# Graph transformer on one core: when output rows are written, and where q and the attention weights stand in PSUM

## The chip, the cores and the metric

The kernel runs on one core of a Trainium2 chip as one program. The metric is the device time of one execution in microseconds (us). Three timed runs of the kernel before gave 2392.58, 2392.24 and 2391.94 us; their median, 2392.24 us, is the time that the change is measured against. The execution that the profiler recorded is a separate one and took longer (below).

## The reference

There are 3327 nodes with 256 features, and an adjacency matrix of 3327 x 3327 with about 16 neighbours in a row. Layer 0 is a single-head graph attention over this matrix. Layers 1 to 3 are transformer layers whose attention is masked by the same matrix (8 heads of 32, feed-forward width 1024):

```python
def layer(x, adj, w_qkv, w_proj, b_proj, w1, b1, w2, b2, g1, be1, g2, be2):
    q, k, v = split(layer_norm(x, g1, be1) @ w_qkv)          # 3 x (n, heads, 32)
    scores = einsum('nhd,mhd->hnm', q, k) * SCALE
    attn = softmax(where(adj != 0, scores, -inf), axis=-1)
    x = x + einsum('hnm,mhd->nhd', attn, v).reshape(n, 256) @ w_proj + b_proj
    return x + gelu(layer_norm(x, g2, be2) @ w1 + b1) @ w2 + b2
```

The output is x after layer 3, in the order of the input's rows.

## The kernel before, in words

Layer 0 reads the whole adjacency matrix, and in passing makes for each node a list of its neighbours. Nodes are then sorted by their number of neighbours and cut into 26 blocks of 128 rows, so that a block needs only as many neighbour places (`CAPS`, 9 to 34) as its fullest row. Everything after that works on the sorted blocks; `perm` holds each row's original number.

Layers 1 to 3 each run over the blocks in the order 24, 23, ..., 0, 25 (`ORDER`). A block's neighbour places are cut into groups of up to four (`cuts`), and one group is one turn: 118 turns in a layer. Five engines share a turn:

- GpSimd (POOL) gathers. `gather` (L759) sends one indirect DMA for each neighbour place: 128 rows of keys and values (2 KB each) from `kv` in HBM to one of 12 slots in SBUF; 430 gathers in a layer. A loop in `layer` (L878) sends them up to four groups ahead of the group in hand, while slots are free.
- VectorE (DVE) multiplies the keys by q (L778), sums over each head (L779), takes the maximum and subtracts it (L785 to L788, in `exps`), and later multiplies the values by the weights (L811).
- ScalarE (ACT) takes the exponent (L789), copies the block's q into PSUM (L757, `place_q`), moves the summed values out (L820) and does the activations of the feed-forward part (L693).
- TensorE (PE) sums the weighted values of a block by transposing them into one PSUM accumulation (L814), and does all projections: `w_proj` (L665), `w1` (L689), `w2` (L702), and q, k, v of the next layer (L183, L188).
- SyncE (SP) loads q (L753, `load_q`) and stores k, v and q for the next layer (L728, L729).

The attention of a block overlaps that of the next one: while block k's scores are made, block k-1 has its softmax shares (`shares`, L791) and its values (`values`, L804). When a chunk of two blocks has its values, a generator `tail` (L652) is put on the list `tails`; each call of `turn` (L827) lets every tail that is due go one step on: projection, addition to x (L668), layer norm, whose power -0.5 is done by POOL (L137), feed-forward, addition to x (L708), and then q, k, v of the next layer.

The order of all this is written out by hand: under `manual_schedule`, each engine's instructions stand in the order in which the Python code issues them, and each engine takes its own queue in order. An instruction that waits therefore holds up all that stands behind it on its engine.

Two places matter here.

First, PSUM for q. The pool `ps_q` has two buffers of one PSUM bank each, and the blocks take turns in them. A block's q is copied into columns 0 to 255 (L757), all its keys are multiplied by it, and then `shares` writes the weights over q in the same columns (L798, L799), where `values` reads them. The buffer is free for block k+2 when block k has all its values. `place_q` of block k+1 is therefore issued when block k-1 has its last values, behind that block's L820, in the last turn but one of block k (L895, L896):

```python
                            if before.vdone == len(before.cuts) and k + 1 < NB:
                                att[k + 1].place_q()
```

Second, the output. In layer 3 a tail ends with the rows of its chunk, two turns after the addition L708 (L710): POOL writes one block after the other with an indirect DMA into `out`, 128 rows of 1 KB, by the row numbers in `perm` (L713). All 26 writes name the whole tensor `out`, so each waits until the one before it has landed. These writes stand in POOL's queue between the gathers: 22 of the 26 ahead of layer 3's last gather, always two in succession.

After layer 3 a few instructions work out a flag (L936) for whether the neighbour lists were large enough; a general path, not run here, would otherwise recompute everything.

Of the kernel before, what the change touches and what calls it, by code (L numbers as in the profile page):

```python
# [8 lines left out]
FP = mybir.dt.float32  # L9
# [6 lines left out]
PSUM = bass.MemoryType.PSUM  # L16
# [37 lines left out]
AHEAD = 3  # L54
NODES = 4
EARLY = 3
FH = FF // P // 2


# [5 lines left out]
def kernel(ctx: ExitStack, tc: tile.TileContext, ins, out: bass.AP):  # L65
# [563 lines left out]
    with ExitStack() as st:  # L629
# [3 lines left out]
        slots = st.enter_context(tc.tile_pool(name="slots", bufs=SLOTS))  # L633
        ps_g = st.enter_context(tc.tile_pool(name="ps2_g", bufs=4, space=PSUM))
        ps_o = st.enter_context(tc.tile_pool(name="ps2_o", bufs=2, space=PSUM))
        ps_q = st.enter_context(tc.tile_pool(name="ps2_q", bufs=2, space=PSUM))

        def gen(name):
            return ps_g.tile([P, 512], FP, tag="g", name=name)

        x_sb = keep.tile([P, NB, D], FP, name="x_sb")
        def node_x(b):
            nc.scalar.copy(x_sb[:, b, :], nodes_[b][:, :D])

# [7 lines left out]
        def tail(L, w, wqn, blocks, oT):  # L652


            n = len(blocks)
            b0 = blocks[0]
            tag = f"{L}_{b0}"
            xi = x_sb[:, b0:b0 + n, :]
            views = [x_sb[:, b, :] for b in blocks]
            pp = gen(f"pp_{tag}").rearrange("p (b d) -> p b d", d=D)  # L660
            nc.tensor.matmul(pp[:, :n, :], ones3,
                             bsum[:, 2 * L - 2, None, :].to_broadcast([3, n, D]), start=True, stop=False)
            for j in range(n):
                for c in range(2):
                    nc.tensor.matmul(pp[:, j, :], oT[:, c, j * P:(j + 1) * P], w["w_proj"][:, c, :],  # L665
                                     start=False, stop=(c == 1 and j == n - 1))
            yield 1
            nc.vector.tensor_add(xi, xi, pp[:, :n, :])  # L668
            mv, rs = variances(views, f"f{tag}")
            yield 2  # L670
            powers(rs, n)
            yield AHEAD - 1
            xns = normed(work, views, mv, rs, f"f{tag}")
            yield 1
            fT = work.tile([P, 2, 2 * P], FP, tag="fT", name=f"fT_{tag}")
            turned(gen, fT, xns, *gains(L, 1), f"f{tag}")
            yield 1
            pd = None
            while hidden:
                yield 1  # L680
            hidden.append(tag)
            for h in range(2):
                gT = work.tile([P, FH, 2 * P], FP, tag="gT", name=f"gT_{tag}_{h}")
                for f0 in range(0, FH, 2):
                    pu = gen(f"pu_{tag}_{h}_{f0}").rearrange("p (a r) -> p a r", a=2)
                    for a in range(2):
                        f = h * FH + f0 + a
                        for c in range(2):
                            nc.tensor.matmul(pu[:, a, :n * P], w["w1"][:, c, f * P:(f + 1) * P],  # L689
                                             fT[:, c, :n * P], start=(c == 0), stop=(c == 1))  # L690
                    for a in range(2):
                        f = h * FH + f0 + a
                        nc.scalar.activation(gT[:, f0 + a, :n * P], pu[:, a, :n * P], AF.Gelu_apprx_tanh,  # L693
                                             bias=pv[:, L - 1, 8 + f:9 + f])
                yield 1
                if h == 0:
                    pd = gen(f"pd_{tag}").rearrange("p (b d) -> p b d", d=D)
                    nc.tensor.matmul(pd[:, :n, :], ones3,
                                     bsum[:, 2 * L - 1, None, :].to_broadcast([3, n, D]), start=True, stop=False)
                for j in range(n):  # L700
                    for f in range(FH):
                        nc.tensor.matmul(pd[:, j, :], gT[:, f, j * P:(j + 1) * P], w["w2"][:, h * FH + f, :],  # L702
                                         start=False, stop=(h == 1 and f == FH - 1 and j == n - 1))
                if h == 0:
                    yield 1
            hidden.remove(tag)
            yield 1
            nc.vector.tensor_add(xi, xi, pd[:, :n, :])  # L708
            if L == LAYERS[-1]:
                yield 2  # L710
                for b in blocks:
                    r = ROWS[b]
                    nc.gpsimd.indirect_dma_start(  # L713
                        out=out, out_offset=bass.IndirectOffsetOnAxis(ap=perm[:r, b:b + 1], axis=0),
                        in_=x_sb[:r, b, :], in_offset=None)
                return
            mv, rs = variances(views, f"h{tag}")
            yield 2
            powers(rs, n)
            yield AHEAD - 1  # L720
            xns = normed(work, views, mv, rs, f"h{tag}")
            yield 1
            hT = work.tile([P, 2, 2 * P], FP, tag="fT", name=f"hT_{tag}")
            turned(gen, hT, xns, *gains(L + 1, 0), f"h{tag}")
            yield 1
            for j, b in enumerate(blocks):
                kv, q = qkv_rows(work, gen, wqn, hT[:, :, j * P:(j + 1) * P], L + 1, f"{L + 1}_{b}")
                nc.sync.dma_start(kv_dr[L + 1][b * P:(b + 1) * P, :], kv)  # L728
                nc.sync.dma_start(q_dr[L + 1][:, b, :], q)  # L729
                if j < n - 1:  # L730
                    yield 1
# [7 lines left out]
        class Attend:  # L739


            def __init__(self, L, b):
                self.L, self.b, self.tag, self.S = L, b, f"{L}_{b}", CAPS[b]
                self.cuts = cuts(b)
                self.tiles = []
                self.vdone = 0

            def load_q(self):
                if self.L == LAYERS[0]:
# [3 lines left out]
                    nc.sync.dma_start(self.q, q_dr[self.L][:, self.b, :])  # L753

            def place_q(self):
                self.qp = ps_q.tile([P, 512], FP, tag="qp", name=f"qp_{self.tag}")
                nc.scalar.copy(self.qp[:, :D], self.q)  # L757

            def gather(self, g):  # L759
                a, z = self.cuts[g]  # L760
# [8 lines left out]
            def scores(self, g):  # L769
                a, z = self.cuts[g]  # L770
                n = z - a
                if g == 0:
                    self.sc = work.tile([P, LW, HEADS], FP, tag="sc", name=f"sc_{self.tag}")
                if self.L == LAYERS[0]:

                    nc.scalar.copy(idx[:, self.b, a:z], self.tiles[g][:, :n, 2 * D])
                kq = self.tiles[g][:, :n, :D]
                nc.vector.tensor_mul(kq, kq, self.qp[:, None, :D].to_broadcast([P, n, D]))  # L778
                nc.vector.tensor_reduce(self.sc[:, a:z, :],  # L779
                                        kq.rearrange("p s (h d) -> p s h d", h=HEADS), AX.X, ALU.add)  # L780

# [9 lines left out]
            def shares(self):  # L791
                S = self.S
                scs = self.sc[:, :S, :]
                sm = work.tile([P, HEADS], FP, tag="sm", name=f"sm_{self.tag}")
                nc.vector.tensor_reduce(sm, scs.rearrange("p s h -> p h s"), AX.X, ALU.add)
                nc.vector.reciprocal(sm, sm)

                self.pw = self.qp[:, :LW * HEADS].rearrange("p (s h) -> p s h", h=HEADS)  # L798
                nc.vector.tensor_mul(self.pw[:, :S, :], scs, sm[:, None, :].to_broadcast([P, S, HEADS]))  # L799
                self.po = ps_o.tile([P, 2, P], FP, tag="po", name=f"po_{self.tag}")  # L800
                nc.tensor.matmul(self.po.rearrange("p c r -> p (c r)"), zeros_bf[:, :P], zeros_bf,
                                 start=True, stop=False)
# [20 lines left out]
        place = {b: (m, j) for m, blocks in enumerate(CHUNKS) for j, b in enumerate(blocks)}  # L823
        tails = []
        hidden = []

        def turn():  # L827

# [7 lines left out]
        def layer(L):  # L836
# [14 lines left out]
            att[0].load_q()  # L851
            att[0].place_q()
            att[1].load_q()
            before = None

            def part(a):
# [10 lines left out]
            for k, a in enumerate(att):  # L867
# [3 lines left out]
                for g in range(n):  # L871
# [10 lines left out]
                    a.scores(g)  # L882
                    if g == n - 1:
                        a.exps()
                    turn()
                    if k == NB - 1:
                        turn()
                    if before is not None:
                        if g == 0:
                            before.shares()  # L890
                        goal = max(g + 1, -(-len(before.cuts) * (g + 1) // max(n - 1, 1)))
                        while before.vdone < min(goal, len(before.cuts)):
                            part(before)
                            held -= 1
                            if before.vdone == len(before.cuts) and k + 1 < NB:  # L895
                                att[k + 1].place_q()  # L896
                    elif g == n - 1:
                        att[1].place_q()
                    now += 1
                before = a  # L900
            before.shares()
            while before.vdone < len(before.cuts):
                part(before)
                turn()
            while tails:
                turn()

        with tc.manual_schedule():
            for L in LAYERS:
# [191 lines left out]
```

## Time and profile before

| | |
|---|---|
| timed runs, median (lowest to highest) | 2392.24 us (2391.94 to 2392.58) |
| the profiled execution, its own time | 2871.28 us |
| its span, first to last instruction | 2869.2 us |
| mean granted TensorE clock in it | 0.753 |
| layer 0 and lists, to the first gather of layer 1 | 411 us |
| gathers of layer 1, first to last | 411 to 1186 us |
| gathers of layer 2 | 1262 to 1988 us |
| gathers of layer 3 | 2067 to 2803 us |
| the end, after the last gather | 67 us |

The profiled execution is 479 us longer than the median of the timed ones. Its durations are read as durations of single instructions; its waits belong to it alone, and how far the timed runs have them too has to be argued.

How to read the lines that follow: a row of the costliest groups gives the source line, the engine, the operation, out<-in, the count, then busy us and mean ns of one, then the idle time of the engine just before these instructions and who ended it. A row of waits gives the engine and line that waited, what released it, the sum in us, how many times, and the longest. A row of a stretch gives its limits, its length, and the busy time of each engine with its number of instructions. A row of the timeline gives start, length, engine, line, operation, and in brackets the idle time before it and who ended it. "issue" means that nothing in the profile explains the idle time; "remote" is a releaser that the trace does not hold.

### The profile page before, as it was taken

The page shows a single profiled execution, that of the slowest core. Times are in us where ns is not written, and L with a number is a line of the kernel's source. Part 1 is how long each engine was busy: PE and PEld are TensorE (multiplying, and loading weights), DVE is VectorE, ACT ScalarE, POOL GpSimd, SP SyncE. Part 2 cuts the span into 40 slices and gives each one's busy share as a digit, 9 for nine tenths or more (in the row PEclk, how much of TensorE's full clock was granted, in tenths as well). Part 3 has the DMA queues.
Part 4 walks back from the last instruction along what each step waited for, and adds up shares of the span by engine and source line. Part 5 has one row for each costly group of instructions (what it writes and reads, how often), then busy time and mean ns, then how long its engine had stood idle before and what let it go on. Part 6 is the DMA issues. An engine that isn't in the chain of part 4 may idle for free.

```text
span 2869.2 us, 26077 instructions
## 1 busy us (share of the span) xinstructions
PE 1716.9 (60%) x8346; PEld 1327.7 (46%) x8346; DVE 1756.5 (61%) x3214; ACT 776.2 (27%) x1564; POOL 1430.0 (50%) x1614
## 2 busy tenths in 40 slices
PE   7677622455666666752576676666725555566556
PEld 6555411444454444642454555554514444444445
DVE  5777735665667776725565755767246467555664
ACT  4777510123322222220232222122302222111112
POOL 0232345554456665336555556664165555665561
PEclk9889855677877667885687777777957777676768
DMA  5667155555456665345545556565255555555451
GB/s 211 218 179 223 59 137 165 151 172 148 129 156 187 178 183 169 109 154 170 148 146 158 174 162 191 169 182 151 99 175 161 155 152 155 168 172 152 145 170 30
DMA packets 165082, 453.04 MB, mean 158 GB/s; under 512 B 37711, under 2 KB 64985, under 8 KB 161609
## 3 DMA queue, kind: packets, MB, share of 16 engines
q0 software_dynamic: 107104, 350.26, 41.8%
q1 hardware_dynamic: 56652, 98.53, 10.9%
q10 hardware_dynamic: 1180, 2.49, 0.3%
q8 instruction: 69, 1.13, 0.2%
q14 instruction: 77, 0.63, 0.1%
HBM read 410.86 MB, written 40.29 MB: 157 GB/s over the span
## 4 chain that ended last, share of the span: by engine, by line
PE 32%; another core or an unknown queue 18%; DVE 17%; issue 15%; ACT 6%; POOL 6%; DMA 5%; DVEq 0%; ACTq 0%; SPq 0%; POOLq 0%
PE pd L702 8%; PE pu L689 7%; PE po L814 5%; PE pk L183 4%; DVE sl L778 4%; DVE sl L811 4%; POOL sl L764 3%; PE pp L665 3%; DVE sc L779 2%; DMA kv<-kvr 2%; DMA sl<-kv,idx 2%; PE pq L188 2%; ACT gT L693 1%; ACT L693 1%
## 5 line engine op out<-in xcount | busy, mean ns | idle before, releaser
L764 POOL DMA_INDIRECT sl<-kv,idx x1290 | 1229.0, 953 | 544.0 <-issue 355.4
L814 PE MATMUL po<-ident,sl 128*128 128x128 f32 x2580 | 471.7, 346 | 568.1 <-DVE sl L811 302.4
L778 DVE TENSOR_TENSOR sl<-sl,qp 128x1024 f32<-128x1024 f32 (+1 forms) x354 | 396.3, 1119 | 568.4 <-ACT qp L757 484.3
L814 PEld LDWEIGHTS po<-ident,sl 128*128 128x128 f32 x2580 | 395.6, 180 | 634.2 <-DVE sl L811 360.3
L702 PE MATMUL pd<-w,gT 128*128 128x256 f32 x1248 | 336.1, 427 | 165.4 <-ACT gT L693 112.6
L779 DVE TENSOR_REDUCE sc<-sl 128x32 f32<-128x1024 f32 (+1 forms) x354 | 398.2, 1125 | 29.5 <-remote 10.5
L689 PE MATMUL pu<-fT,w 128*128 128x256 f32 (+1 forms) x1344 | 328.6, 402 | 127.9 <-issue 66.4
L811 DVE TENSOR_TENSOR sl<-sl,qp 128x1024 f32<-128x1024 f32 (+1 forms) x354 | 388.9, 1119 | 8.1 <-DVE qp L799 3.5
L702 PEld LDWEIGHTS pd<-w,gT 128*128 128x128 f32 x1248 | 261.2, 215 | 228.0 <-ACT gT L693 127.1
L689 PEld LDWEIGHTS pu<-fT,w 128*128 128x128 f32 x1344 | 266.0, 213 | 176.2 <-issue 72.3
L693 ACT ACTIVATE gT<-pu,pv 128x256 f32<-128x256 f32 (+1 forms) x336 | 133.1, 456 | 374.5 <-remote 175.3
L137 POOL TENSOR_TENSOR rsig_f<-rsig_f,mhalf 128x2 f32<-128x2 f32 (+1 forms) x42 | 29.1, 693 | 339.6 <-DVE rsig_f L133 337.6
L820 ACT COPY oT<-po 128x256 f32<-128x256 f32 x78 | 29.1, 373 | 617.3 <-remote 228.6
L183 PE MATMUL pk<-wq,hT 128*128 128x512 f32 x312 | 169.6, 670 | 19.8 <-ACT hT L165 18.6
L708 DVE TENSOR_TENSOR x_sb<-x_sb,pd 128x512 f32<-128x512 f32 (+1 forms) x42 | 27.2, 648 | 207.2 <-PE pd L702 144.9
L608 DVE MAX8 cand<-abf 128x8 f32<-128x256 bf16 x338 | 118.2, 411 | 1.3 <-DMA node<-cand 1.1
L665 PE MATMUL pp<-w_proj,oT 128*128 128x256 f32 x312 | 94.1, 452 | 35.6 <-ACT oT L820 26.3
L165 ACT ACTIVATE fT<-pn_f,pv 128x256 f32<-128x256 f32 (+1 forms) x84 | 41.6, 545 | 249.2 <-remote 155.1
L693 ACT ACT_TABLE_LOAD x48 | 61.6, 1283 | 151.9 <-remote 88.4
L183 PEld LDWEIGHTS pk<-wq,hT 128*128 128x128 f32 x312 | 61.6, 215 | 71.8 <-issue 42.6
L185 ACT COPY kvr<-pk 128x512 f32<-128x512 f32 x78 | 46.0, 589 | 180.5 <-PE pk L183 125.5
L137 POOL TENSOR_TENSOR rsig_h<-rsig_h,mhalf 128x2 f32<-128x2 f32 (+1 forms) x28 | 19.5, 695 | 146.3 <-DVE rsig_h L133 118.2
(220 smaller groups left out, 1999.7 us busy)
## 6 DMA issues: line engine op xcount, KB each, us to landing
a<-in_adj_dram SPq DMA_DIRECT2D x25, 1663.5 KB
sl<-kv,idx POOLq DMA_INDIRECT x1290
kv<-kvr SPq DMA_DIRECT2D x78, 256.0 KB
q<-qr SPq DMA_DIRECT2D x52, 128.0 KB
q<-q SPq DMA_DIRECT2D x52, 128.0 KB
w<-in_L_gnn_w_dram SPq DMA_DIRECT2D x6, 1024.0 KB
node<-x SPq DMA_DIRECT2D x26, 128.0 KB
node<-qr SPq DMA_DIRECT2D x26, 128.0 KB
```

The lines of the kernel that those rows point to most:

```text
L183: nc.tensor.matmul(pk, hT[:, c, :], wq[:, c, D:], start=(c == 0), stop=(c == 1))
L188: nc.tensor.matmul(pq[:, :D], hT[:, c, :], wq[:, c, :D], start=(c == 0), stop=(c == 1))
L608: nc.vector.max(out=cand[:, 8 * m:8 * m + 8], in_=ab3[:, m, :])
L665: nc.tensor.matmul(pp[:, j, :], oT[:, c, j * P:(j + 1) * P], w["w_proj"][:, c, :], start=False, stop=(c == 1 and j == n - 1))
L689: nc.tensor.matmul(pu[:, a, :n * P], w["w1"][:, c, f * P:(f + 1) * P], fT[:, c, :n * P], start=(c == 0), stop=(c == 1))
L693: nc.scalar.activation(gT[:, f0 + a, :n * P], pu[:, a, :n * P], AF.Gelu_apprx_tanh, bias=pv[:, L - 1, 8 + f:9 + f])
L702: nc.tensor.matmul(pd[:, j, :], gT[:, f, j * P:(j + 1) * P], w["w2"][:, h * FH + f, :], start=False, stop=(h == 1 and f == FH - 1 and j == ...
L764: nc.gpsimd.indirect_dma_start(out=t[:, k - a, :w], out_offset=None, in_=kv_dr[self.L][:, :], in_offset=bass.IndirectOffsetOnAxis(ap=idx[: ...
L778: nc.vector.tensor_mul(kq, kq, self.qp[:, None, :D].to_broadcast([P, n, D]))
L779: nc.vector.tensor_reduce(self.sc[:, a:z, :], kq.rearrange("p s (h d) -> p s h d", h=HEADS), AX.X, ALU.add)
L811: nc.vector.tensor_mul(vv, vv, self.pw[:, a:z, :, None].to_broadcast([P, n, HEADS, HD]))
L814: nc.tensor.matmul(self.po[:, c, :], t[:, k, D + c * P:D + (c + 1) * P], ident, is_transpose=True, start=False, stop=(a + k == self.S - 1 ...
```

## The change

It has two parts.

The output. A tail of layer 3 no longer writes. One turn after the addition L708 it puts its blocks on a list, `ended`. A new function `write(most)` sends the write of up to `most` blocks from the head of that list. The turn loop calls `write(1)` in each turn in which all gathers of the layer have been sent, or more than `LATE` = 12 blocks are on the list; the loops after the last turn call `write(1)` in each of their turns, and `write(NB)` at the very end. Counted in the built program, 10 writes then stand ahead of layer 3's last gather and 16 behind it. The ten stand singly, with three gathers or more between one and the next; the 16 stand as 1, 4, 4 and 7, parted by the three last powers (L137).

q and weights. Two PSUM tiles of one bank each are made once, and the blocks take turns in them. q has columns 0 to 255; the weights have the last 256 columns (the last 272 for block 0, whose weights need 272), so they no longer lie over q, save for 16 columns in block 0. `place_q` of block k+2 is issued right after `exps` of block k, in that block's last turn, and `place_q` of the second block at the layer's start.

In the built program the instructions of PE, DVE and SP stand in the order of before. On ACT the 78 copies L757 are moved; on POOL the 26 writes are. Among the waits, three kinds change. The first key product of a block (L778) no longer waits for ACT. The write of the weights (L799) now waits for ACT, which means for the copy of q that was just issued into the same bank, for the block after the next one. In layer 1 each first gather into a reused slot names ACT among its waits beside DVE and PE.

```diff
+LATE = 12
...
-        ps_q = st.enter_context(tc.tile_pool(name="ps2_q", bufs=2, space=PSUM))
+        ps_q = st.enter_context(tc.tile_pool(name="ps2_q", bufs=1, space=PSUM))
...
+        qws = [ps_q.tile([P, 512], FP, name=f"qw{k}") for k in range(2)]
...
             if L == LAYERS[-1]:
-                yield 2
-                for b in blocks:
-                    r = ROWS[b]
-                    nc.gpsimd.indirect_dma_start(
-                        out=out, out_offset=bass.IndirectOffsetOnAxis(ap=perm[:r, b:b + 1], axis=0),
-                        in_=x_sb[:r, b, :], in_offset=None)
+                yield 1
+                ended.extend(blocks)
                 return
...
+                w = qws[ORDER.index(b) % 2]
+                self.qp = w[:, :D]
+                self.pw = w[:, 512 - max(D, self.S * HEADS):512].rearrange("p (s h) -> p s h", h=HEADS)
...
             def place_q(self):
-                self.qp = ps_q.tile([P, 512], FP, tag="qp", name=f"qp_{self.tag}")
-                nc.scalar.copy(self.qp[:, :D], self.q)
+                nc.scalar.copy(self.qp, self.q)
...
-                self.pw = self.qp[:, :LW * HEADS].rearrange("p (s h) -> p s h", h=HEADS)
...
+        def write(most):
+
+            for b in ended[:most]:
+                r = ROWS[b]
+                nc.gpsimd.indirect_dma_start(
+                    out=out, out_offset=bass.IndirectOffsetOnAxis(ap=perm[:r, b:b + 1], axis=0),
+                    in_=x_sb[:r, b, :], in_offset=None)
+            del ended[:most]
...
             att[1].load_q()
+            att[1].place_q()
...
                     if g == n - 1:
                         a.exps()
+
+                        if k + 2 < NB:
+                            att[k + 2].place_q()
                     turn()
                     if k == NB - 1:
                         turn()
+                    if sent == turns or len(ended) > LATE:
+                        write(1)
...
-                            if before.vdone == len(before.cuts) and k + 1 < NB:
-                                att[k + 1].place_q()
-                    elif g == n - 1:
-                        att[1].place_q()
...
             while before.vdone < len(before.cuts):
                 part(before)
                 turn()
+                write(1)
             while tails:
                 turn()
+                write(1)
+            write(NB)
```

More of the change, by code (lines that the diff above doesn't have):

```diff
@@ L777, in scores @@
                 kq = self.tiles[g][:, :n, :D]
-                nc.vector.tensor_mul(kq, kq, self.qp[:, None, :D].to_broadcast([P, n, D]))
+                nc.vector.tensor_mul(kq, kq, self.qp[:, None, :].to_broadcast([P, n, D]))
                 nc.vector.tensor_reduce(self.sc[:, a:z, :],
@@ L825 @@
         hidden = []
+        ended = []
+        def write(most):
[5 more added lines that the diff above has]
+            del ended[:most]
         def turn():
```

## The prediction, as it was put on record

> **What bounds the kernel now.** I read the page first, its shares and its costliest groups:
>
> ```profile
> PE 1716.9 (60%) x8346; PEld 1327.7 (46%) x8346; DVE 1756.5 (61%) x3214; ACT 776.2 (27%) x1564; POOL 1430.0 (50%) x1614
> L764 POOL DMA_INDIRECT sl<-kv,idx x1290 | 1229.0, 953 | 544.0 <-issue 355.4
> L778 DVE TENSOR_TENSOR sl<-sl,qp 128x1024 f32<-128x1024 f32 (+1 forms) x354 | 396.3, 1119 | 568.4 <-ACT qp L757 484.3
> ```
>
> No engine is full, and VectorE alone waits 484.3 us for the copy of q (L757), the wait that the change takes away. Next, DVE's waits over the whole span, to see what stands behind that one:
>
> ```profile
> DVE sl L778 <- ACT qp L757: 484.3, 37, 23.5
> DVE x_sb L708 <- PE pd L702: 144.9, 27, 15.3
> DVE x_sb L668 <- PE pp L665: 91.5, 28, 7.8
> ```
>
> Then the timeline of one such wait, at the start of layer 2:
>
> ```profile
> 1292.19 1.09 PE L814 MATMUL po<-ident,sl 128*128 128x128 f32 x8 [1.56 <-DVE sl L811]
> 1293.22 0.28 PE L801 MATMUL po<-zeros_bf 1*128 1x256 bf16 x1
> 1317.37 0.37 ACT L820 COPY oT<-po 128x256 f32<-128x256 f32 x1 [33.30 <-remote]
> 1317.64 0.38 ACT L757 COPY qp<-q 128x256 f32<-128x256 f32 x1
> 1318.06 1.22 DVE L778 TENSOR_TENSOR sl<-sl,qp 128x1024 f32<-128x1024 f32 x1 [22.62 <-ACT qp L757]
> ```
>
> TensorE's last transposes of that block end at 1293.3 us and its queue then stands empty, yet ACT's copy of their sum, which waits for PE alone, starts 24 us later. Nothing in the program explains this, so I take much of the 484 us for a thing of the profiled execution. How much, POOL's queue tells. Its three gather streams and the end, by stretches (after the length the busy us of PE, weight loads, DVE, ACT and POOL, then TensorE's clock, DMA share, GB/s):
>
> ```profile
> 411.10:1186.00 774.90, 441.13 (x1864) 337.89 (x1864) 508.58 (x964) 179.96 (x479) 446.09 (x475) 0.72 0.56 166
> 1262.00:1988.50 726.50, 441.85 (x1864) 339.11 (x1864) 449.33 (x637) 159.28 (x317) 425.33 (x452) 0.74 0.59 175
> 2066.60:2802.60 736.00, 388.24 (x1665) 307.67 (x1665) 439.62 (x579) 120.91 (x237) 439.91 (x463) 0.70 0.56 165
> 2802.60:2869.20 66.60, 46.30 (x270) 39.38 (x270) 23.85 (x41) 16.07 (x40) 7.45 (x7) 0.86 0.06 17
> ```
>
> Gathers in succession start 1.25 us apart (0.95 and an "issue" gap of 0.30; 355 us of such gaps on the page). POOL's own time is then, for layer 1, 430 gathers and 22 node loads x 1.25 and 23 powers x 1.02 (0.72 + 0.30): 588. Layer 2: 430 x 1.25 + 22 x 1.02 = 560. Layer 3: 430 x 1.25 + 11 x 1.02 + 48 for writes (below) = 597. Over these sums the streams took 187 + 167 + 139 = 493 us in which POOL waited. The timed runs are 2871.3 - 2392.2 = 479 us shorter. If in them POOL hardly waits inside a stream, the time comes out as 2871.3 - 493 = 2378, within 14 us of the median. So I take the timed runs to be **bound by POOL's queue** within a layer; DVE's 509, 449 and 440 us and PE's 441, 442 and 388 lie below 588, 560 and 597.
>
> Last, what POOL waits for in layer 3's stream, and in the timeline one pair of writes:
>
> ```profile
> POOL rsig_f L137 <- DVE rsig_f L133: 72.7, 6, 14.3
> POOL out_dram L713 <- DVE x_sb L708: 32.8, 5, 9.9
> POOL out_dram L713 <- DMA out_dram<-x_sb,perm: 22.7, 11, 2.7
> ```
>
> ```profile
> 2720.44 1.01 POOL L713 DMA_INDIRECT out_dram<-x_sb,perm  x1 [0.30 <-DVE mx L787]
> 2723.53 0.98 POOL L713 DMA_INDIRECT out_dram<-x_sb,perm  x1 [2.08 <-DMA out_dram<-x_sb,perm]
> 2724.82 0.99 POOL L764 DMA_INDIRECT sl<-kv,idx  x1 [0.31 <-issue]
> ```
>
> The second write of each pair holds POOL until the first has landed.
>
> **What the Trainium skill says.** "Perfetto Trace Analysis", section on the per-instruction lifecycle: TensorE's ends in a profile are estimated, and GpSimd's spans are better read from start to start. The 24 us above and the 1.25 us against 0.95 agree. "DMA: Bandwidth & Descriptors", section on the anatomy of one DMA (gpsimd path): about 2.0 us fixed plus bytes / 436e3, mostly the receipt of the last write; for 128 KB an estimate of 2.3 us. The trace has a wait of 22.7 / 11 = 2.06 us after the first write's issue: it agrees. "PSUM — Partial Sum Buffer", section on bank collisions: two engines must be kept apart by bank, not by address. That is why the built program still orders the weights (L799) after a copy of q into other columns of the bank; no run here shows a collision.
>
> **The change part by part.** *Writes ahead of layer 3's last gather.* Before: 22 x 0.994 = 21.9 us issuing, 11 waits for landing = 22.7 us, 11 plain gaps x 0.30 = 3.3 us; 47.9 in all. After: 10 single writes x 1.29 = 12.9 us; three gathers or more (3.8 us) lie between two of them, longer than the 2.75 us from write to write that a landing takes, so no wait is left. Each writes a block of a chunk finished long before, so the 32.8 us of waits for L708 go too. I count those at nothing: a POOL that waits for L708 is ahead of DVE and would wait at its next power or slot instead. Gain **35.0 us** of POOL's queue (the upper end for that reason; 0 the lower, if DVE or PE is late anyway).
>
> *Writes behind it.* 16 instead of 4, each now after the one before has landed: 2.75 us (2835.96 to 2838.71 in the end of before). They pass three powers that gate the last tails. In the profiled end the power of block 0 is wanted at 2823.6 and that of block 25 at 2838.6. POOL does a write, a power and 4 writes by 2815, then waits; 4 more start from 2824.7 and end at 2834: neither power is late. Then 7, from 2839.5: the seventh, block 25's, at 2839.5 + 6 x 2.75 = 2856.0, against 2855.2 before. Cost **+0.8 us** (0 to +6, if the timed end is shorter).
>
> *q placed ahead.* 78 copies of 0.38 us stay on ACT, moved behind the exponent. L778 no longer waits for them. What is late next: in the same turn DVE comes to L708 or L668, which wait for PE (144.9 and 91.5 us already), and then to the sum of shares (L795), which needs the exponent that stands behind the same L820 on ACT. DVE can move ahead only L778 and L779, 2.24 us, of a wait of 13. With POOL late, DVE's lead buys nothing: **0** (to -14, the rest that POOL's sums leave). If the timed runs waited as the profile does: in 27 of the 37 waits, by the timeline, L668 or L708 follows in the same turn and nothing is won; in 10 it is 2 us: -20.
>
> *The new wait*, L799 on ACT: behind it on DVE stand all later value and key products, and PE for the values. The copy follows the exponent at once and takes 0.38 us; DVE has the sum and reciprocal (0.5 us) in between: 0. Without that cover 78 x 0.38 = 30 us. q must have landed: in the trace its load is issued 16 us or more ahead of that point. The added ACT waits in layer 1's gathers are for copies made eight turns earlier: 0 (to +3).
>
> Sum: -35.0 + 0.8 = -34.2. Against the profiled execution's own 2871.3 (span 2869.2 and 2.1 around it) that gives 2837.1, if its waits allowed it; but there POOL isn't late, and less will show. Against the median, which is the execution that I argue to be bound by POOL: 2392.2 - 34.2 = **2358.0 us**.
>
> **The rivals.** *As profiled.* The timed runs wait as the profile does, only less: POOL's saving is swallowed by DVE's and PE's waits, and the q part wins its 20 us: 2392.2 - 20 + 0.8 = 2373. For it: POOL waited 139 us in that stream. Against: the 479 us. *Swallowed altogether.* DVE's next wait ends where the old one did, and DVE or PE limits layer 3: 2392.2 - 1 = 2391. *More.* The 14 us that the POOL sums leave are such waits for q, and go too: 2358 - 14 = 2344. *Slower.* One mechanism: the chain of 16 writes behind the last gather, each held by the landing before. With s us from write to write the last one starts about 15 s after that gather, against 52.6 before (2855.2 - 2802.6); at 2.75 the chain is hidden but for its last step. If it runs at 5, it starts at 75, +23, and if POOL's saving is swallowed down to 12 us elsewhere: 2392 - 12 + 23 = 2403. It decides from 15 s = 52.6 + 12, s = 4.3. Against: the landings took 1.7 to 2.7 us beside gathers, and the end has almost no other traffic (17 GB/s). That the columns stay coupled (the bank is ordered as a whole) is true and costs nothing, as above.
>
> **How the numbers follow.** POOL bound 0.60 (2350 to 2370), as profiled 0.17, more 0.05, swallowed 0.10, slower 0.08. About 0.2% (5 us) is what a measurement here can tell from no change. Faster by that: 0.60 + 0.17 + 0.05 = 0.82; within: 0.10; slower: 0.08. The range 2342 to 2388 leaves out the slower case and most of the swallowed one.
>
> **What would show it.** In the profile after: L778 without waits for ACT, and DVE's waits gone over to L668, L708 and L795; no pair of writes ahead of the last gather, and fewer than 15 us of POOL's time on them; layer 3's stream shorter than layer 2's; behind it writes 2.7 us apart and a last one within 3 us of the last addition. It is wrong if layer 3's stream keeps its length, or if layers 1 and 2, which the writes do not touch, change by more than a few us: then the q part was the one that counted.

## The result, and the profile after

The changed kernel takes 2354.26 us (median of four runs, 2347.69 to 2359.77) against 2392.09 us for the kernel before: a ratio of 0.9855, 95% interval 0.9833 to 0.9877, or 29 to 40 us less. The forecast was 2358.0 us. The profiled execution of after took 2350.96 us, with a span of 2349.1 us and a mean granted clock of 0.802.

One fact must be known ahead of all the numbers below. The time of this program depends on the chip: the kernel before takes 2384 to 2392 us on some chips and 2870 to 2872 us on others, in timed runs as in profiled ones. By its time and its clock (2871.28 us, 0.753) the profile of before that the prediction read came from a chip of the longer kind, and that of after (2350.96 us, 0.802) from one of the shorter kind. So the two profiles can't be laid side by side stretch by stretch. Each ratio here is between kernels run on the same chip, and stretches are compared between chips of one kind.

First the busy shares and the costliest groups of after, from its page:

```profile
PE 1619.5 (69%) x8346; PEld 1278.3 (54%) x8346; DVE 1758.5 (75%) x3214; ACT 778.9 (33%) x1564; POOL 1430.9 (61%) x1614
L767 POOL DMA_INDIRECT sl<-kv,idx x1290 | 1228.6, 952 | 410.4 <-issue 311.7
L781 DVE TENSOR_TENSOR sl<-sl,qw 128x1024 f32<-128x1024 f32 (+1 forms) x354 | 396.4, 1120 | 170.9 <-DMA sl<-kv,idx 86.8
```

DVE and POOL are busy for as long as before (1758.5 and 1430.9 us against 1756.5 and 1430.0); PE's 1716.9 us have become 1619.5 at a higher clock. The key product (L781 now, L778 before) waits 170.9 us in place of 568.4, and no longer for q in the main. DVE's waits by what released them:

```profile
DVE x_sb L713 <- PE pd L707: 185.8, 32, 10.4
DVE sl L781 <- DMA sl<-kv,idx: 86.8, 69, 3.1
DVE sl L781 <- ACT qw L760: 43.2, 2, 23.7
DVE x_sb L673 <- PE pp L670: 34.8, 20, 6.9
```

What is left for ACT's copy of q are two waits with 43.2 us together. Against the 37 waits and 484.3 us of before this looks like a large gain, and the experiments below show that it is none. The stretches of after (length, busy us of PE, weight loads, DVE, ACT and POOL, clock, DMA share, GB/s) are the three gather streams and the end:

```profile
417.80:1012.10 594.30, 405.68 (x1864) 319.03 (x1864) 509.24 (x966) 181.40 (x479) 446.36 (x475) 0.79 0.75 216
1086.60:1650.00 563.40, 405.20 (x1864) 318.71 (x1864) 451.58 (x640) 160.72 (x317) 425.49 (x453) 0.80 0.76 225
1724.60:2285.40 560.80, 361.18 (x1674) 295.01 (x1675) 449.06 (x585) 121.96 (x238) 428.08 (x451) 0.74 0.74 213
2285.40:2349.10 63.70, 45.22 (x263) 38.44 (x261) 18.72 (x35) 15.24 (x38) 19.19 (x19) 0.88 0.13 43
```

Layer 3's stream is shorter than layer 2's. Within it POOL's groups (busy us, mean ns, idle before them) are these:

```profile
L767 POOL DMA_INDIRECT sl<-kv,idx x430 | 409.7, 953 | 138.8 <-issue 103.5 <-DMA sl<-kv,idx 13.7 <-DMA q<-qr 9.1
L833 POOL DMA_INDIRECT out_dram<-x_sb,perm x10 | 10.4, 1035 | 2.7 <-issue 2.1 <-DMA sl<-kv,idx 0.3 <-DVE sc L782 0.3
L139 POOL TENSOR_TENSOR rsig_f<-rsig_f,mhalf 128x2 f32<-128x2 f32 x11 | 8.1, 733 | 0.2
```

These three rows add up to 409.7 + 138.8 + 10.4 + 2.7 + 8.1 + 0.2 = 569.9 us. Less the 9.1 us of waiting for the last store of q (`q<-qr`), which lie ahead of the first gather and so of the stretch, that is 560.8, the whole stream. The gaps ahead of gathers are (138.8 - 9.1) / 430 = 0.30 us each: POOL sends one instruction after the other and hardly waits for anybody. The ten writes take 10.4 + 2.7 = 13.1 us, without one wait for a landing.

### The profile page after: what moved, and what is told of

It reads as the page before. It is cut to its first block, busy times and chain, and to the rows that moved or that the text cites. A ratio compares the mean times of both kernels' runs of the same rounds, so it can differ in the third digit from the quotient of the medians.

```text
span 2349.1 us, 26111 instructions
## 1 busy us (share of the span) xinstructions
PE 1619.5 (69%) x8346; PEld 1278.3 (54%) x8346; DVE 1758.5 (75%) x3214; ACT 778.9 (33%) x1564; POOL 1430.9 (61%) x1614
## 3 DMA queue, kind: packets, MB, share of 16 engines
q0 software_dynamic: 107104, 350.26, 51.8%
## 5 line engine op out<-in xcount | busy, mean ns | idle before, releaser
L815 PE MATMUL po<-ident,sl 128*128 128x128 f32 x2580 | 465.7, 344 | 505.2 <-DVE sl L812 479.3
L815 PEld LDWEIGHTS po<-ident,sl 128*128 128x128 f32 x2580 | 393.0, 179 | 568.4 <-DVE sl L812 557.0
L781 DVE TENSOR_TENSOR sl<-sl,qw 128x1024 f32<-128x1024 f32 (+1 forms) x354 | 396.4, 1120 | 170.9 <-DMA sl<-kv,idx 86.8
L812 DVE TENSOR_TENSOR sl<-sl,qw 128x1024 f32<-128x1024 f32 (+1 forms) x354 | 388.9, 1119 | 2.7
L694 PE MATMUL pu<-fT,w 128*128 128x256 f32 (+1 forms) x1344 | 297.7, 377 | 9.6 <-ACT fT L167 9.6
L707 PE MATMUL pd<-w,gT 128*128 128x256 f32 x1248 | 288.8, 384 | 0.9 <-ACT gT L698 0.9
L694 PEld LDWEIGHTS pu<-fT,w 128*128 128x128 f32 x1344 | 248.0, 198 | 42.8 <-ACT fT L167 12.1
L707 PEld LDWEIGHTS pd<-w,gT 128*128 128x128 f32 x1248 | 232.7, 191 | 38.4 <-ACT gT L698 4.8
L713 DVE TENSOR_TENSOR x_sb<-x_sb,pd 128x512 f32<-128x512 f32 (+1 forms) x42 | 27.2, 647 | 185.9 <-PE pd L707 185.8
L600 ACT ACTIVATE aT<-pt 128x1024 bf16<-128x1024 bf16 x104 | 85.5, 874 | 8.1 <-PE pt L599 7.9
L190 PEld LDWEIGHTS pq<-wq,hT 128*128 128x128 f32 x312 | 61.6, 197 | 46.5 <-issue 38.4
L603 PE MATMUL pa<-hs,aT 128*128 128x193 bf16 x676 | 78.4, 270 | 8.0 <-ACT aT L600 7.5
```

Of the source, the lines that this page charges most:

```text
L600: nc.scalar.activation(aT[:, k0:k0 + kn, :], pt[:, :kn, :], AF.Sign)
L781: nc.vector.tensor_mul(kq, kq, self.qp[:, None, :].to_broadcast([P, n, D]))
L812: nc.vector.tensor_mul(vv, vv, self.pw[:, a:z, :, None].to_broadcast([P, n, HEADS, HD]))
L815: nc.tensor.matmul(self.po[:, c, :], t[:, k, D + c * P:D + (c + 1) * P], ident, is_transpose=True, start=False, stop=(a + k == self.S - 1 ...
```

## The experiments

"Output part" and "q part" name the two halves of the change. Lengths of streams are from the first gather of a layer to its last.

### Is the long profile a thing of profiling?

The kernel before was run again, unchanged, with timed runs beside the profile (e1).

> The kernel before, unchanged, profiled once more. If the 479 us by which its first profiled execution was longer belong to that execution alone, this one comes out near 2392 us, its three gather streams within 15 us of POOL's own sums (588, 560 and 597 us), and the first key products wait little for the copy of q. If they belong to the kernel under the profiler, the execution is again near 2870 us and the streams near 775, 727 and 736.

It took 2873.16 us in timed runs, beside another set of timed runs of itself on that chip at 2871.78 (0.9995, 0.9974 to 1.0016), and 2868.6 us by its profile, at a clock of 0.750. The streams were 774.0, 724.8 and 734.6 us, as in the profile of before. So the 479 us are not a cost of being profiled: the timed runs on this chip have them too. The waits for q are as they were, and behind them stand two others:

```profile
DVE sl L778 <- ACT qp L757: 509.7, 38, 23.6
DVE x_sb L708 <- PE pd L702: 145.2, 27, 17.2
DVE x_sb L668 <- PE pp L665: 89.6, 29, 7.1
```

### Each part alone, on two chips of the longer kind

The output part alone (e2, and e5 on the second chip) is the kernel before with this core of the change:

```diff
-                yield 2
-                for b in blocks:
-                    ...
+                yield 1
+                ended.extend(blocks)
...
+                    if sent == turns or len(ended) > LATE:
+                        write(1)
```

> The kernel before with the output part of the change alone; q and weights stay as they were. If POOL's queue is the bound: 35.0 us less in layer 3's stream and 1.8 us more at the end, 2359 us, ratio 0.986. If the placing of q is what counts, the writes give little: 2375 to 2392 us.

> The output part alone, run once more, because the first runs fell on a chip on which the kernel before takes 2872 us. Where the kernel before takes 2392 us and POOL's queue is the bound: 35.0 us less in layer 3's stream, 1.8 us more at the end, 2359 us, ratio 0.986. If the placing of q is what counts there: 2375 to 2392 us. On the slower chip again: ratio 0.996.

e2 took 0.9960 (0.9940 to 0.9981) of the time before, e5 0.9966 (0.9945 to 0.9988): 9 and 11 us less. In the profiles layer 3's stream went from 734.6 us (e1) to 716.7 (e2) and 699.8 (e5). These are single executions: that of e2 is the longest of its 22, that of e5 one of the shortest of its 17. The last write started 62.5 us after the last gather in e2 and 55.7 in e5, against 51.8 in e1, so part of what the stream won was lost again at the end.

Most of POOL's saving did not even reach the stream. POOL's writes and powers in layer 3's stream, first in e1, then in e2:

```profile
L713 POOL DMA_INDIRECT out_dram<-x_sb,perm x22 | 21.9, 997 | 61.7 <-DVE x_sb L708 36.1 <-DMA out_dram<-x_sb,perm 23.8 <-issue 1.2
L137 POOL TENSOR_TENSOR rsig_f<-rsig_f,mhalf 128x2 f32<-128x2 f32 x11 | 8.0, 731 | 70.1 <-DVE rsig_f L133 69.9
```

```profile
L831 POOL DMA_INDIRECT out_dram<-x_sb,perm x10 | 10.2, 1016 | 2.8 <-issue 2.4 <-DVE sc L785 0.3
L139 POOL TENSOR_TENSOR rsig_f<-rsig_f,mhalf 128x2 f32<-128x2 f32 x11 | 7.9, 722 | 112.4 <-DVE rsig_f L135 99.1 <-DVE sm L795 13.3
```

The writes went from 21.9 + 61.7 = 83.6 us to 10.2 + 2.8 = 13.0, but POOL's wait ahead of the powers went from 70.1 to 112.4, and its idle time ahead of gathers from 171.1 to 182.0. A POOL that doesn't wait at a write comes to its next power earlier, and waits there for DVE.

The q part alone (e3, and e6 on the second chip) is the changed kernel with the writes put back:

```diff
-                yield 1
-                ended.extend(blocks)
+                yield 2
+                for b in blocks:
+                    ...
...
-                    if sent == turns or len(ended) > LATE:
-                        write(1)
```

> The kernel before with the q and weights part alone; the output rows are written in pairs as before. If POOL's queue is the bound: 0 to 5 us less, 2387 to 2392 us, ratio 0.998 to 1.000 (what the measured 37.8 us leave over the 33.2 us of the writes is 4.6 us). If the placing of q is what counts: 20 us less or more, 2372 us or below, ratio 0.992 or below.

> The q and weights part alone, once more for the same reason. Where the kernel before takes 2392 us and POOL's queue is the bound: 0 to 5 us less, ratio 0.998 to 1.000. If the placing of q is what counts: 20 us less or more, ratio 0.992 or below. On the slower chip again: ratio 1.000.

e3 took 0.9998 (0.9971 to 1.0026) and e6 1.0028 (1.0009 to 1.0048): nothing, or a little slower. The 20 us that the rival "as profiled" gave to the q part do not come even where the waits for q are long. DVE's waits in e3 show why:

```profile
DVE x_sb L713 <- PE pd L707: 323.3, 28, 25.8
DVE x_sb L673 <- PE pp L670: 290.6, 27, 25.6
DVE sl L785 <- ACT qw L764: 44.7, 2, 23.9
```

Against e1 the wait for q went from 509.7 to 44.7 us, and the two waits of the additions for PE from 145.2 + 89.6 = 234.8 to 323.3 + 290.6 = 613.9 us. One place in layer 1 shows how. In e1 ACT waits 16.39 us ahead of the feed-forward activation L693 (with the load of its table), which reads PE's product; the trace doesn't hold the releaser. q's copy L757 stands behind it on ACT's queue, DVE's key product waits for that copy, and the addition L668 then for PE. In e3, in the same turn, DVE waits at the addition (L673 there) alone:

```profile
596.04 1.28 ACT L693 ACT_TABLE_LOAD   x1 [16.39 <-remote]
599.03 0.41 ACT L757 COPY qp<-node 128x256 f32<-128x256 f32 x1
599.48 0.95 DVE L778 TENSOR_TENSOR sl<-sl,qp 128x768 f32<-128x768 f32 x1 [11.39 <-ACT qp L757]
605.91 0.69 DVE L668 TENSOR_TENSOR x_sb<-x_sb,pp 128x512 f32<-128x512 f32 x1 [4.49 <-PE pp L665]
```

```profile
603.73 0.69 DVE L673 TENSOR_TENSOR x_sb<-x_sb,pp 128x512 f32<-128x512 f32 x1 [14.73 <-PE pp L670]
```

Two waits of 11.39 + 4.49 = 15.88 us have become one of 14.73. The wait was named after q's copy because that copy stood behind the real wait on ACT's queue.

One more was run on the first chip: the changed kernel with no deferral, in which a block is written as soon as it is on the list (e4).

```diff
-LATE = 12
+LATE = 0
```

> The changed kernel with LATE 0: each block is written, singly, in the turn after it ends; 22 writes ahead of layer 3's last gather and 4 behind it, as in the kernel before, but none in a pair. If POOL's queue is the bound, 12 more single writes of 1.29 us stand in the stream than in the changed kernel and the end is 1.8 us shorter: 2354 + 15.5 - 1.8 = 2368 us, ratio 0.990; so the splitting of pairs is worth 19.5 us and the deferring 13.7. If deferring is all the gain, it is back near 2385.

It took 1.0095 (1.0068 to 1.0122): slower than before. A block comes to be written one turn after the addition L713 and not two, and POOL waited for that addition ten times, 56.7 us. But the 22 writes ahead of the last gather took 81.2 us in all, no more than the 83.6 of e1, so these waits alone don't explain the loss. In the profile layer 3's stream is 16.5 us longer than in e1, and the last write starts 61.7 us after the last gather and not 51.8; the cause stays open. On a chip of this kind the output part gained with the deferral (e2, e5), and without it the kernel lost (e4, which has the q part too).

### Where POOL sets the time: the same parts with less work on PE

To see POOL's bound without PE's delays, part of PE's work in layers 1 to 3 was left out in four kernels, which therefore don't compute the reference: one of the two halves of `w1`, three products in four of `w2`, and one of the two halves of each value row. In layer 1's stream 1044 of 1864 matmuls are left.

```diff
-                        for c in range(2):
-                            nc.tensor.matmul(pu[:, a, :n * P], w["w1"][:, c, f * P:(f + 1) * P],
-                                             fT[:, c, :n * P], start=(c == 0), stop=(c == 1))
+                        nc.tensor.matmul(pu[:, a, :n * P], w["w1"][:, 0, f * P:(f + 1) * P],
+                                         fT[:, 0, :n * P], start=True, stop=True)
...
-                    for f in range(FH):
...
-                    for c in range(2):
```

They ran on one chip of the shorter kind, on which the kernel before took 2386.29 us: the kernel before with this edit (e7), with the output part (e8), with the q part (e9), and with both (e10).

> The kernel before with about half of TensorE's work in layers 1 to 3 left out (one of two 128-row halves in the first feed-forward product, one of four in the second, one of two halves of each value row in the transposes), all else as it was, POOL's queue to the instruction. If POOL's queue is the bound once TensorE keeps up: layer streams within 15 us of POOL's sums (588, 560, 597 us) and a time of 2365 to 2395 us also on a chip where the full kernel takes 2870 us. If the time there comes from POOL, DMA or DVE, or from waits for q that have nothing to do with TensorE: well above 2450 us.

> The same leaving-out, with the output part of the change alone. If POOL's queue is the bound: 33 us less than the light kernel before (35.0 less in layer 3's stream, 2 more at the end), and nothing in layers 1 and 2. If the writes do not lie on the path: within 5 us of it.

> The same leaving-out, with the q and weights part alone. If POOL's queue is the bound: 0 to 5 us less than the light kernel before. If the wait for q at each block's start is what holds the kernel: 20 us less or more.

> The same leaving-out, with both parts. If POOL's queue is the bound: 33 to 38 us less than the light kernel before, the sum of the two parts. If the parts help one another (a DVE freed from the wait for q feeds a POOL freed from the writes): clearly more than the sum.

| | time, us (lowest to highest) | layer 3's stream | last write, us after the last gather |
|---|---|---|---|
| e7, neither part | 2313.44 (2308.33 to 2315.65) | 600.6 | 33.6 |
| e8, output part | 2285.27 (2282.06 to 2287.61) | 560.5 | 46.9 |
| e9, q part | 2310.13 (2306.89 to 2316.48) | 597.7 | 33.6 |
| e10, both | 2283.36 (2279.29 to 2291.22) | 560.7 | 46.2 |

The output part is worth 28.2 us here, the q part 3.3 us with ranges that overlap, both together 30.1. The 33 us that were expected of the output part did not come in full: the stream gave 40.1, but the end took 13 and not 2. The stretches of e7:

```profile
419.10:1002.60 583.50, 294.62 (x1044) 191.59 (x1045) 516.31 (x976) 185.22 (x485) 447.84 (x475) 0.68 0.75 220
1057.00:1612.50 555.50, 293.64 (x1044) 192.11 (x1045) 461.08 (x651) 161.56 (x322) 426.53 (x452) 0.69 0.76 228
1665.10:2265.70 600.60, 257.22 (x856) 170.24 (x856) 451.82 (x588) 121.88 (x238) 440.95 (x463) 0.61 0.69 202
2265.70:2313.60 47.90, 24.02 (x115) 17.21 (x113) 15.95 (x32) 14.89 (x38) 7.48 (x8) 0.79 0.08 23
```

PE is busy 294.6 us of layer 1's stream where after has 405.7, and the stream is only 594.3 - 583.5 = 10.8 us shorter. That is what a bound by POOL looks like: over a quarter of another engine's work in a stretch goes, and the stretch all but stays. The prediction's sums of POOL's own time (588, 560, 597) lie within 5 us of these three. The expected time of e7, 2365 to 2395 us, was missed all the same (2313.44). From after to e10, the same kernel but for PE's work on two chips of the shorter kind, the span falls by 71.2 us: the three streams give 12.2, 9.2 and 0.0, the stretches between the layers 40.2, the rest lies ahead of layer 1's stream and at the end. So POOL sets the streams, and PE has a large part in what lies between them.

This group also shows the rival that was to end slower. The end of e7 and that of e10, POOL's last instructions (start, length, then the idle time and what ended it):

```profile
2293.34 1.03 POOL L711 DMA_INDIRECT out_dram<-x_sb,perm  x1 [3.29 <-DVE x_sb L706]
2299.28 2.56 POOL L711 DMA_INDIRECT out_dram<-x_sb,perm  x1 [4.91 <-DVE x_sb L706]
```

```profile
2256.48 0.97 POOL L829 DMA_INDIRECT out_dram<-x_sb,perm  x1 [2.60 <-DMA out_dram<-x_sb,perm]
2259.99 0.97 POOL L829 DMA_INDIRECT out_dram<-x_sb,perm  x1 [2.54 <-DMA out_dram<-x_sb,perm]
2263.36 2.56 POOL L829 DMA_INDIRECT out_dram<-x_sb,perm  x1 [2.39 <-DMA out_dram<-x_sb,perm]
```

In e7 the last write waits for the last addition. In e10 that addition ends at 2253.34 us, ten ahead of the last write, which waits for the landing of the one before: the chain of 16 is the end. The last write comes 46.2 - 33.6 = 12.6 us later after the last gather than in e7. Of these 9.7 are the chain: the last write starts 10.44 us after the last addition's start in e10 and 0.74 in e7. The other 2.9 are an addition that itself comes later. The stream had won 39.9.

### The full work on a chip of the shorter kind

The q part alone with all of PE's work (e11) and the changed kernel with `LATE = 0` (e12) ran on one more chip of that kind, on which the kernel before took 2384.29 us.

> The q and weights part alone, with all of TensorE's work. Where the kernel before takes about 2390 us, the light kernels say 3 us less (2313.4 to 2310.1); the change as a whole gained 37.8 us and the writes are sized at 33 to 38: 0 to 5 us less, ratio 0.998 to 1.000, and layer 3's stream still near 600 us. If the light kernels hid q's wait together with TensorE's work: 10 us less or more, ratio 0.996 or below. Where the kernel before takes 2870 us: ratio 1.000, as in two runs already.

> The changed kernel with LATE 0: every block written singly, 22 ahead of layer 3's last gather and 4 behind it. Where the kernel before takes about 2390 us: 15.5 us more in the stream than in the changed kernel (560.8, so 576) and about 2 less at the end, ratio 0.990 against the kernel before; so the splitting of pairs is worth some 20 us and the deferring 13. If a write one turn after the addition makes POOL wait for DVE, the stream is back near 600 and the ratio near 0.998. Where the kernel before takes 2870 us: ratio 1.0095, as measured.

e11 took 2387.26 us: 1.0008 (0.9994 to 1.0021). It writes as before does, and since before itself was not profiled on such a chip, e11 stands in for it. e12 took 2366.82 us: 0.9939 (0.9915 to 0.9962). The four stretches of e11:

```profile
416.70:1015.50 598.80, 408.65 (x1864) 321.06 (x1864) 509.66 (x966) 181.94 (x479) 447.61 (x474) 0.78 0.72 214
1090.00:1653.40 563.40, 406.09 (x1864) 319.05 (x1864) 451.77 (x640) 161.09 (x317) 426.67 (x452) 0.79 0.75 225
1728.00:2327.30 599.30, 366.63 (x1690) 298.81 (x1691) 451.55 (x588) 122.14 (x238) 441.20 (x463) 0.74 0.69 202
2327.30:2385.80 58.50, 41.72 (x248) 34.79 (x245) 15.88 (x32) 15.30 (x38) 7.50 (x8) 0.90 0.07 20
```

And its writes within layer 3's stream, then those of e12:

```profile
L718 POOL DMA_INDIRECT out_dram<-x_sb,perm x22 | 21.9, 997 | 28.5 <-DMA out_dram<-x_sb,perm 20.5 <-ACT sc L796 4.6 <-issue 2.7
```

```profile
L833 POOL DMA_INDIRECT out_dram<-x_sb,perm x22 | 22.4, 1019 | 6.3 <-issue 4.4 <-DVE sc L782 0.9 <-DMA sl<-kv,idx 0.6
```

In pairs the 22 writes take 21.9 + 28.5 = 50.4 us; singly, 22.4 + 6.3 = 28.7; and ten of them, 13.1. The stream follows nearly one for one: 599.3, then 577.5 (e12), then 560.8 us (after). So the gain has two halves: parting the pairs is worth 21.7 us of POOL's time and 21.8 of the stream, and moving twelve writes behind the last gather 15.6 and 16.7. These are three single executions; by the medians of the timed runs on the one chip e12 is 20.4 us faster than e11.

What the second half costs is at the end. POOL's last power in after, the first of the seven writes behind it, and the last three:

```profile
2316.33 0.57 POOL L139 TENSOR_TENSOR rsig_f<-rsig_f,mhalf 128x1 f32<-128x1 f32 x1 [2.78 <-DVE rsig_f L135]
2317.11 1.03 POOL L833 DMA_INDIRECT out_dram<-x_sb,perm  x1 [0.20 <-issue]
2327.85 0.97 POOL L833 DMA_INDIRECT out_dram<-x_sb,perm  x1 [1.71 <-DMA out_dram<-x_sb,perm]
2331.19 0.97 POOL L833 DMA_INDIRECT out_dram<-x_sb,perm  x1 [2.37 <-DMA out_dram<-x_sb,perm]
2334.55 2.55 POOL L833 DMA_INDIRECT out_dram<-x_sb,perm  x1 [2.39 <-DMA out_dram<-x_sb,perm]
```

The last addition starts at 2332.05 us in after and at 2371.10 in e11, which is 46.65 and 43.80 us after the last gather. The last write starts 2.50 us behind it in after (held by the landing before) and 0.74 us in e11 (held by DVE alone).

## Why the prediction was right, step by step

**The bound: right, by a wrong reason.** Within a layer POOL's queue sets the time on the chips of the shorter kind. Beside the sums of 588, 560 and 597 us the streams were 598.8, 563.4 and 599.3 (e11), and leaving out part of PE's work moved them by 12.2, 9.2 and 0.0 us (after against e10). But the prediction reached this by taking much of the waits for q for "a thing of the profiled execution". They are a thing of the kind of chip: timed runs on such a chip are as long as the profile, whose waits they therefore share (e1). The step from the 479 us to the POOL bound held because it compared POOL's own work, which is the same on both kinds of chip, with the time of the very runs that the forecast was for.

**Writes ahead of the last gather, -35.0: right.** Their time went from 50.4 to 13.1 us, 37.3, against the predicted 47.9 to 12.9. The stream gave 38.5. The lower end, 0, was far off here; on the other kind of chip the output part is worth 9 to 11 us in all. The 32.8 us of waits for L708, which the prediction counted at nothing, were not there on the shorter kind (none in e11's stream); on the longer kind they did move to the next power, as it said (e2).

**The end, +0.8 (0 to +6): the right mechanism, the size too small.** The last write started 44.54 us after the last gather in e11 and 49.15 in after: 4.6 us more. Of that 1.76 us (2.50 - 0.74) are the chain, and 2.85 (46.65 - 43.80) are a last addition that comes later.

The chain's part is the forecast term and a little more. The last power waits 2.78 us for DVE and not for a write, so the count begins anew behind it, as the prediction had it. With 2.75 us a step the seventh write would start at 2317.11 + 6 x 2.75 = 2333.61 us, and without a chain, as in e11, at 2332.05 + 0.74 = 2332.79: 0.8 us. But the last two steps took 3.34 and 3.36 us, which adds 0.9; why they did was not found. A bare step takes 2.68 us (2322.50 to 2325.18), near the 2.75 of the prediction; the estimate of 2.3 us that it worked out from the Trainium skill's "DMA: Bandwidth & Descriptors" (section on the anatomy of one DMA) is 0.4 short of it, and 0.2 short of the 2.5 us that the trace of after gives as the median from a write's issue to its landing. With two waits for powers and some longer landings between them, the 16 take (2334.55 - 2285.69) / 15 = 3.26 us each on average.

The later addition has no term in the prediction. It shows wherever the writes are parted: 46.3 us after the last gather in e12 and 46.7 in after, against 43.8 in e11; 35.8 in e8 and e10, against 32.8 and 32.9 in e7 and e9. The likely reason is that POOL has gained on the rest, which then has more left to do at the last gather; this was not tried by itself.

**q placed ahead, 0: right.** 1.0008 (0.9994 to 1.0021) with all of PE's work, and at most the 3.3 us of e9 with less. On the longer kind of chip too a wait of 465 us vanished without a gain. "What is late next" was named rightly: on that kind of chip 379.1 us of the waits went to the two additions (613.9 - 234.8), and the sum of shares waited 66.3 us in e3 where it had waited 0.0 in e1. In after, on the shorter kind, it waited 0.0.

**The new wait on ACT, 0: right.** Without the q part the write of the weights is idle for 2.7 us in e7, with it for 8.0 in e9 and in after, over 78 blocks: 5.3 us in all, on an engine that isn't the bound. The added waits in layer 1 don't show: on one chip its stream is 582.1 us with them (e9 and e10), and 583.5 and 581.8 without (e7 and e8).

**The signs.** No pair is left ahead of the last gather, the writes there take 13.1 us (under 15), layer 3's stream is shorter than layer 2's (560.8 against 563.4), and the last write starts 2.08 us after the last addition's end. The writes behind the last gather are 2.7 us apart only in their bare steps. That DVE's waits went over can be seen only on the longer kind (e3), since before has no profile on the shorter. Layer 2 stands at 563.4 us in both e11 and after; layer 1 differs by 4.5 us, which nothing in the output part explains and which single executions can't settle (e12 has 594.6).

**The sum.** From e11 to after, span for span: -38.5 in layer 3's stream, +5.2 at the end, -4.5 in layer 1's stream, +1.1 ahead of it: -36.7. Forecast, -34.2; measured between medians, -37.8. That the two lie so close is in part luck: the end cost 4.4 us more than forecast, the stream won 3.5 more, and 3.4 more came from stretches that the writes don't touch.

**The rivals.** *As profiled* describes the other kind of chip half: POOL's saving is mostly swallowed there (9 to 11 us of 35 are left), but its 20 us for q were wrong. *Slower* is a real mechanism that costs the full kernel only 1.8 us: with a shorter end (e10) the same chain loses 9.7. *Swallowed* and *more* did not come.

**Open.** Why the chips differ was not found, and since each chip was used in one session, chip and session can't be told apart. The changed kernel itself was not run on a chip of the longer kind; only its parts and e4 were. The output part alone was not run with PE's full work on the shorter kind; that it is all of the gain there rests on the q part giving nothing (e11) and on the light kernels (e8 beside e10). Writing without the order between the rows of `out`, which might shorten the chain, was not tried. No version here that computes the reference is faster than the changed kernel.

## What to carry to other kernels

Ahead of crediting a removed wait, ask what its engine meets next in the same turn: here some 500 us of waits named after one copy came from the PE that this copy stood behind, and taking them away gave nothing. Where the profiled execution is far from the timed ones, first see whether the two were taken on the same chip. Then add up each in-order queue's own time from start to start, and compare the sums with the timed runs. Here POOL's sum filled the streams of the timed kernel, and what was taken out of its queue came back nearly one for one in the stream. Where other engines were late, POOL's next wait took most of it. Writes to one tensor that follow each other by landing took 1.3 us each when they stood apart and 2.3 in pairs; moved to the end they are free only while the end's other work is longer than their chain.

## What the hardware showed that was not expected

The same program took 2384 to 2392 us on some chips and 2870 to 2872 us on others, with a mean granted TensorE clock of 0.80 and 0.75. The clock seems to explain little: PE's busy time differs by 1719.4 (e1) - 1619.5 (after) = 100 us, the whole time by about 480. On the longer kind ACT and DVE start up to 24 us after the modelled end of the PE work that they wait for. On the shorter kind the longest wait of an addition for PE was 10.4 us, against 25.8 in e3. The Trainium skill's "Perfetto Trace Analysis" (section on the per-instruction lifecycle) says that TensorE's ends are estimated; that agrees with such gaps, but it can't be all of it, since the timed runs on these chips are as long as the profiled ones. Where the time goes within PE's work is not shown by any run.
